# Two visits to half-size TensorE tiles per group of four batches become one

## The chip, the cores and the metric

The kernel runs on one core of a Trainium2 chip. A time is the device time of one launch in microseconds (us), the median of several runs; less is better. A core has five engines that work side by side, each through its own queue of instructions in the order of the program: TensorE (PE; its weight loads are listed as PEld), VectorE (DVE), ScalarE (ACT), GpSimd (POOL) and SyncE (SP), which here issues every DMA. Engines wait for each other with semaphores. TensorE writes into PSUM, which has eight banks; VectorE and ScalarE empty them.

## The reference

`x` is 128 batches of 128 nodes with 512 features, `adj` a 128 x 128 weighted adjacency matrix. Two layers follow each other, each with a residual. All is fp32.

```python
# layer 0
h = relu(layernorm(x))
x = x + (adj @ h) @ L0_weight + L0_bias
# layer 1: attention of 8 heads of 64, masked where adj == 0
h = relu(layernorm(x))
q, k, v = split(h @ w_qkv)
attn = softmax(where(adj == 0, -inf, q @ k.T * 64 ** -0.5))
o = (attn @ v) @ w_proj + b_proj
x = x + o + layernorm(o) * gamma + beta
```

## The kernel before

**Two phases.** Phase 1 (`phase1`, L479) does layer 0 for all batches and puts x1 and x1 + beta into DRAM. Phase 2 (`phase2_group`, L569) does layer 1 in 32 groups of four batches, each group two pairs. Weight products are made of three fp32r matmuls (high part, low part, correction) for precision: `times_weights` (L449) has 12 matmuls of 128x512 for one batch, and writes two PSUM banks, a and b.

**A group of phase 2** has on TensorE:
- qk (L594): eight blocks of 12 matmuls over all four batches; ScalarE (L601) and VectorE (L602) bring banks a and b together into `qk` tiles;
- v: 12 matmuls for each batch (L455 with `wv`), emptied at L629 and L630;
- scores (L651): 8 fp32 matmuls for each batch with a contraction of 64, so two row halves of the array work side by side. They fill two banks for each batch. VectorE adds the mask (L660) and takes maxima (L665), ScalarE the exponentials (L672), VectorE the reciprocals (L677), GpSimd divides (L678);
- the probabilities go to DRAM and back with rows exchanged (`exchange`, L521), and VectorE transposes blocks (L703);
- attend (L721): 8 fp32 matmuls for each batch with 64 output rows, two column halves of the array; one bank for each batch;
- `split_left` (L441) cuts an attend bank into three parts (ScalarE L443, VectorE L444 and L445), and proj multiplies them: 12 matmuls for each batch (L455 with `wA`); then bias, layernorm and residual, and a store.

The attends of a group take place in the next group. Scores and attends both use the array in halves. Before, each group goes to half-size tiles twice: attends of the older group's first pair with scores of this group's first pair, then, later in the group, the same for the second pairs. `rests` holds what is left to do for each pair: `rest_of` gives the read-back, transposes, attend, proj and the tail of the layer.

**The next group's hidden states** are fetched meanwhile (`fetch`, L537): read x1, statistics, relu (L553), to DRAM and back, transposes (L557), then the three parts on ScalarE (L560, L563) and GpSimd (L561, L564). There are six places for batches in `hp`.

**What sets the order.** Every operation goes into a planner (`Plan`, L57) with its engine, an assumed duration, the buffers it reads and writes, and a wanted time: `at` for TensorE, `due` for the others. The planner runs a list schedule: an engine that is free takes the available operation with the earliest wanted time for which a buffer slot is free, and instructions are emitted in that order. Operations with `tiled=True` are those in half-size tiles: the planner favours staying in the present mode (`stay`) and adds `turn` at a change. Slots are places in SBUF (`t`, `f`) or PSUM banks (`b0` to `b7`, taken by anything named `ps`). `s` (scores) and `pT` (transposed probabilities) share four places f0 to f3. `T4` is the period of a group assumed for the wanted times; `t0` is the start of one. `rank` counts pairs from the end: ranks 1 and 0 are the last group's, rank 0 transposes its probabilities on TensorE (L709) rather than through DRAM, and both use a plain fp32 proj (L740).

Of the kernel before, what the change touches and what calls it, by code (L numbers as in the profile page):

```python
# [52 lines left out]
class Op:  # L53
    __slots__ = ("eng", "us", "fn", "at", "due", "prio", "bufs", "preds", "succ", "n", "ready", "start", "end", "id", "lands", "what", "tiled", "early")


class Plan:  # L57
# [10 lines left out]
    def op(self, eng, us, fn, r=(), w=(), at=None, due=None, lands=None, what="", after=(), tiled=False, early=0.0):  # L68
        o = Op()
        o.eng, o.us, o.fn, o.at, o.due, o.lands, o.what, o.tiled = eng, us, fn, at, due, lands, what, tiled  # L70
        o.early = early
# [30 lines left out]
    def schedule(self):  # L102
# [22 lines left out]
        while len(order) < len(self.ops):  # L125
# [6 lines left out]
            for e in self.ENGINES:  # L132
# [7 lines left out]
                for item in sorted(avail[e], key=lambda i: (i[0] - (stay if self.ops[i[1]].tiled == tiled else 0.0), i[1])):  # L140
                    o, taken = self.ops[item[1]], []
                    if held and any(b.slots in held for b in o.bufs if b.slots and not b.name):
                        continue
# [68 lines left out]
def kernel(  # L212
# [36 lines left out]
    def named(prefix, *numbers):  # L249
# [8 lines left out]
        "qk": group(named("t", 0, 8)), "v": group(named("t", 8, 14)), "op": group(named("t", 14, 18)),  # L258
# [182 lines left out]
    def split_left(p, name):  # L441
        h, l, s = (buf(name, [P, C, P], HALF) for _ in range(3))
        op("ACT", 0.53, lambda: nc.scalar.activation(h.ap, p.ap, AF.Copy, scale=CUT), r=[p], w=[h], what=name + "h")  # L443
        op("DVE", 0.63, lambda: nc.vector.tensor_tensor(l.ap, p.ap, h.ap.bitcast(F32), op=ALU.subtract), r=[p, h], w=[l], what=name + "l")  # L444
        op("DVE", 0.63, lambda: nc.vector.scalar_tensor_tensor(s.ap, h.ap.bitcast(F32), UP, p.ap, op0=ALU.mult, op1=ALU.subtract),  # L445
           r=[p, h], w=[s], what=name + "s")
        return h, l, s

    def times_weights(parts, w, at, what):  # L449
# [7 lines left out]
        for m, (p, start, stop) in enumerate(((a, True, False), (a, False, True), (b, True, True))):  # L457
            op("PE", 0.91, lambda p=p, m=m, start=start, stop=stop: run(p, m, start, stop), r=[parts[m][:2], w], w=[p], at=at + 0.91 * m, what=what)
# [62 lines left out]
    def exchange(src, w, kb, what):  # L521
        d = in_dram([P, Q, w], f"d{w}")
        dma(lambda: d.ap, lambda: src(), kb, r=[src.b], w=[d], what=what + " out")

        def land(dst, after=()):
            for q in range(Q):
                dma(lambda q=q: dst()[q * R:(q + 1) * R, :, :], lambda q=q: d.ap[:, q, :].rearrange("(n r) w -> r n w", n=Q),
                    kb / 4, r=[d], w=[(dst.b, q)], what=what + " in", after=after)
# [40 lines left out]
    def phase2_group(j):  # L569
# [3 lines left out]
        at_qk = (0.0, 2.8, 8.4, 11.2, 16.8, 19.6, 22.4, 25.2)  # L573
        at_v = (31.7, 34.5, 42.9, 45.7)
        at_t = (28.0, 48.5)
        at_p = (37.3, 40.1, 52.3 + 5.6, 52.3 + 14.0)
        if not left:
            at_v, at_t = (31.7, 34.5, 46.6, 49.4), (28.0, 37.3)
        for p in range(2):
            fetch(group[2 * p:2 * p + 2], t0 - (37, 8)[p])  # L580
# [6 lines left out]
        for g in range(8):  # L587
# [15 lines left out]
            if g == 4:  # L603
                gate = [b.writers[-1][1]]
        V = {}

        def scores(p):
            pair = group[2 * p:2 * p + 2]
            at_scores = t0 + at_t[p] + 1.8
# [3 lines left out]
            if rank < 4:  # L613
                last = START2 + T4 * (B // 4 - 1)
                at_attend = [last + d for d in ((66.9, 67.9), (57.8, 57.8), (37.3, 37.3), (28.0, 28.0))[rank]]
                at_proj = [last + d for d in ((69.0, 72.5), (60.0, 63.6), (52.2, 55.0), (41.0, 43.8))[rank]]
            S, last = scores_of(pair, place, QK, rank, at_scores)
            rests.append(lambda gate: rest_of(pair, V, rank, S, at_attend, at_proj, gate))
            final[:] = [last]
            return [last]  # L620

        if rests:
            rests.pop(0)(gate)
        scores(0)
        for n, i in enumerate(group):
            v = V[i] = buf("v", [P, D])
            tv = t0 + at_v[n]
            a, b = times_weights([(HP[i, m], None, part(i, m)) for m in range(3)], wv, tv, "v")
            op("ACT", 0.53, lambda v=v, a=a: nc.scalar.activation(v.ap, a.ap, AF.Copy, scale=UP), r=[a], w=[v], due=tv + 1, what="vA")  # L629
            op("DVE", 0.63, lambda v=v, b=b: nc.vector.tensor_tensor(v.ap, b.ap, v.ap, op=ALU.add), r=[b], w=[v], due=tv + 2, what="vB")  # L630
        if len(rests) > 1:
            rests.pop(0)(gate)
        scores(1)
# [6 lines left out]
    def scores_of(pair, place, QK, rank, at_scores):  # L640

        S = []
        for n, i in enumerate(pair):
            ts = at_scores + 1.0 * n
            ps = [buf("ps", [P, C, P]) for _ in range(2)]
# [13 lines left out]
            for e in range(2):  # L659
# [3 lines left out]
                   r=[ps[e], maskb], w=[(s, e)], due=ts + 1 + n, what="mask")  # L663
            mx = buf("mx", [P, 2 * H])
            op("DVE", 1.15, lambda heads=heads, mx=mx: nc.vector.tensor_reduce(mx.ap[:, :H], heads(), AX.XY, ALU.max),  # L665
               r=[s], w=[mx], due=ts + 4 + 4 * n, what="max")
            op("ACT", 0.2, lambda mx=mx: nc.scalar.mul(mx.ap[:, :H], mx.ap[:, :H], -scale), w=[mx], due=ts + 5 + 5 * n, what="mx")  # L667
# [5 lines left out]
            for g in range(4):  # L673
                op("ACT", 0.79, lambda g=g, exps=exps: exps((2 * g, 2 * g + 1)), r=[(mx, "m")], w=[(s, ("e", g)), (mx, g)],
                   due=ts + 6 + 2.3 * g + 9.2 * n if rank > 1 else ts + 4 + 1.2 * g + 4 * n, what="exp")
            if rank:
                op("DVE", 0.18, lambda mx=mx: nc.vector.reciprocal(mx.ap[:, H:], mx.ap[:, H:]), w=[mx], what="rec", due=ts + (15 + 9.2 * n if rank > 1 else 9 + 4 * n))  # L677
# [3 lines left out]
                   r=[mx], w=[s], what="div", due=ts + (16 + 9.2 * n if rank > 1 else 10 + 4 * n))  # L681
# [9 lines left out]
            land = exchange(View(s, lambda ap: ap), H * R, 512, "e") if rank else None  # L691
# [3 lines left out]
    def rest_of(pair, V, rank, S, at_attend, at_proj, gate):  # L695

        PT = []
        for n, (s, heads, land) in enumerate(S):
            pT = buf("pT", [P, Q, 2 * C, R])
            PT.append(pT)  # L700
            if rank:
                land(View(pT, lambda ap: ap.rearrange("p q h r -> p q (h r)")), gate)
# [13 lines left out]
        def attend(some):  # L716
            for n in some:
# [100 lines left out]
```

## Time and profile before

| | |
|---|---|
| median of 3 runs | 2150.61 us (2149.41 to 2150.62) |
| profiled execution | 2148.78 us, span of its instructions 2147.0 us |
| TensorE busy | 2135.3 us, granted clock 0.999 |
| VectorE, ScalarE, GpSimd busy | 1723.9, 1484.8, 1529.3 us |
| first qk of phase 2 | 475.9 us after the start of the span |
| one group in the steady part | 51.74 us |

Busy time is the union of an engine's instructions. The page also follows the chain of work that ended last, back from the last instruction, and gives its shares by engine and line. A timeline row has start in us from the start of the span, length in us, engine, line, operation, output<-inputs by the program's names, shape and count; instructions of one kind that follow each other are one row. In brackets stands the engine's idle time before it and what ended it. A row of busy times by stretch has, for each engine, the time in which it worked in this stretch and the number of its instructions. An fp32 matmul leaves two records, an fp32r matmul one. Ends of matmuls are modelled; starts of weight loads show the pace better.

### The profile page before, as it was taken

The page shows a single profiled execution, that of the slowest core. Times are in us where ns is not written, and L with a number is a line of the kernel's source. Part 1 is how long each engine was busy: PE and PEld are TensorE (multiplying, and loading weights), DVE is VectorE, ACT ScalarE, POOL GpSimd, SP SyncE. Part 2 cuts the span into 40 slices and gives each one's busy share as a digit, 9 for nine tenths or more (in the row PEclk, how much of TensorE's full clock was granted, in tenths as well). Part 3 has the DMA queues.
Part 4 walks back from the last instruction along what each step waited for, and adds up shares of the span by engine and source line. Part 5 has one row for each costly group of instructions (what it writes and reads, how often), then busy time and mean ns, then how long its engine had stood idle before and what let it go on. Part 6 is the DMA issues. An engine that isn't in the chain of part 4 may idle for free.

```text
span 2147.0 us, 40973 instructions
## 1 busy us (share of the span) xinstructions
PE 2135.3 (99%) x12819; PEld 1781.8 (83%) x12819; DVE 1723.9 (80%) x3279; ACT 1484.8 (69%) x4238; POOL 1529.3 (71%) x1278
## 2 busy tenths in 40 slices
PE   9999999999999999999999999999999999999998
PEld 7888888888888888888888888888888888888885
DVE  7889888886787887787777787777777777777778
ACT  7778778767766666676666666666666666666654
POOL 7888878784666666677777777777777777777655
PEclk9999999999999999999999999999999999999999
DMA  7676666665666666566666666666666666666653
GB/s 241 220 243 227 229 220 226 224 237 163 190 191 185 188 182 179 177 177 177 177 177 177 187 177 179 186 186 195 186 195 185 185 187 185 185 185 184 186 166 108
DMA packets 297865, 410.71 MB, mean 191 GB/s; under 512 B 33072, under 2 KB 163248, under 8 KB 297648
## 3 DMA queue, kind: packets, MB, share of 16 engines
q1 hardware_dynamic: 297648, 408.09, 62.6%
q8 instruction: 102, 1.67, 0.3%
q14 instruction: 115, 0.94, 0.2%
HBM read 207.68 MB, written 200.28 MB: 190 GB/s over the span
## 4 chain that ended last, share of the span: by engine, by line
PE 96%; DVE 1%; DMA 1%; SPq 1%; issue 0%; POOL 0%; ACT 0%; POOLq 0%; DVEq 0%; ACTq 0%
PE b L455 47%; PE b L594 32%; PE b L651 6%; PE b L721 5%; PE b L497 5%; PE b L506 1%; SPq L280 1%; DMA f<-d 0%; DMA f<-in_x_dram 0%; DVE t L756 0%; DMA out_dram<-t 0%; DMA t<-in_x_dram 0%; DVE n L665 0%; DVE t L466 0%; POOL m L397 0%
## 5 line engine op out<-in xcount | busy, mean ns | idle before, releaser
L455 PE MATMUL b<-wA,t 128*128 128x512 f32 x2976 | 732.6, 393 | 1.2 <-DVE t L444 0.8
L594 PE MATMUL b<-hp,wqk 128*128 128x512 f32 x3072 | 715.4, 390 | 0.0
L594 PEld LDWEIGHTS b<-hp,wqk 128*128 128x128 f32 x3072 | 574.3, 188 | 122.1
L455 PEld LDWEIGHTS b<-wA,t 128*128 128x128 f32 x2976 | 549.6, 188 | 110.2 <-DVE t L444 1.0
L561 POOL TENSOR_TENSOR hp<-t,hp 128x512 fp32r<-128x512 f32 x128 | 165.6, 1305 | 400.1 <-ACT hp L560 370.7
L672 ACT ACTIVATE f<-f,n 128x128 f32<-128x128 f32 x1024 | 397.7, 391 | 3.1
L455 PE MATMUL b<-wv,hp 128*128 128x512 f32 x1536 | 378.1, 392 | 0.0
L455 PEld LDWEIGHTS b<-wv,hp 128*128 128x128 f32 x1536 | 285.8, 188 | 62.3
L602 DVE TENSOR_TENSOR t<-b,t 128x512 f32<-128x512 f32 x256 | 175.2, 685 | 137.7 <-PE b L594 74.2
L678 POOL TENSOR_TENSOR f<-f,n 128x1024 f32<-128x1024 f32 x126 | 241.7, 1922 | 57.3 <-DVE n L677 52.2
L601 ACT ACTIVATE t<-b 128x512 f32<-128x512 f32 x256 | 151.4, 592 | 163.4 <-PE b L594 162.9
L444 DVE TENSOR_TENSOR t<-b,t 128x512 fp32r<-128x512 f32 x248 | 168.3, 679 | 64.1 <-ACT t L443 62.8
L672 ACT ACTIVATION_READ_ACCUMULATOR f<-f,n 128x1 f32 x1024 | 194.6, 190 | 0.0
L667 ACT ACTIVATE n<-n 128x8 f32<-128x8 f32 x128 | 26.0, 203 | 241.7 <-DVE n L665 241.7
L703 DVE STREAM_TRANSPOSE f<-f 128x1024 f32<-128x1024 f32 x126 | 156.2, 1239 | 41.0 <-DMA f<-d 37.5
L748 POOL TENSOR_TENSOR t<-t,t 128x512 f32<-128x512 f32 x126 | 164.3, 1304 | 28.7 <-DVE t L466 26.3
L660 DVE TENSOR_TENSOR f<-b,maskb 128x512 f32<-128x512 f32 x256 | 163.7, 680 | 21.7 <-PE b L651 21.7
L443 ACT ACTIVATE t<-b 128x512 fp32r<-128x512 f32 x248 | 144.8, 584 | 47.6 <-PE b L497 42.1
L564 POOL TENSOR_TENSOR hp<-hp 128x512 fp32r<-128x512 f32 x128 | 166.3, 1300 | 5.0
L445 DVE SCALAR_TENSOR_TENSOR t<-t,b 128x512 fp32r<-128x512 f32 x248 | 167.4, 675 | 0.0
L751 POOL TENSOR_TENSOR t<-t,gamma_b 128x512 f32<-128x512 f32 x122 | 158.6, 1300 | 6.0 <-ACT t L750 2.8
L752 POOL TENSOR_TENSOR t<-t,t 128x512 f32<-128x512 f32 x122 | 158.4, 1299 | 5.0
(123 smaller groups left out, 3259.1 us busy)
## 6 DMA issues: line engine op xcount, KB each, us to landing
d<-f SPq DMA_DIRECT2D x126, 512.0 KB, 3.5
f<-d SPq DMA_DIRECT2D x504, 128.0 KB, 4.1
t<-x1d SPq DMA_DIRECT2D x128, 256.0 KB, 3.9
d<-t SPq DMA_DIRECT2D x128, 256.0 KB, 3.7
t<-d SPq DMA_DIRECT2D x512, 64.0 KB, 3.5
t<-x1b SPq DMA_DIRECT2D x128, 256.0 KB, 4.2
out_dram<-t SPq DMA_DIRECT2D x128, 256.0 KB, 3.1
t<-in_x_dram SPq DMA_DIRECT2D x91, 256.0 KB, 3.0
```

The source lines that it names most:

```text
L444: op("DVE", 0.63, lambda: nc.vector.tensor_tensor(l.ap, p.ap, h.ap.bitcast(F32), op=ALU.subtract), r=[p, h], w=[l], what=name + "l")
L445: op("DVE", 0.63, lambda: nc.vector.scalar_tensor_tensor(s.ap, h.ap.bitcast(F32), UP, p.ap, op0=ALU.mult, op1=ALU.subtract), r=[p, h], w=[ ...
L455: nc.tensor.matmul(p.ap, lhsT=parts[m][2]()[:, c], rhs=w.ap[:, m, c, :], start=start and c == 0, stop=stop and c == C - 1)
L561: op("POOL", 1.35, lambda ht=ht, h=h, l=l: nc.gpsimd.tensor_tensor(l(), ht(), h().bitcast(F32), op=ALU.subtract), r=[h1, HP[i, 0]], w=[HP[ ...
L564: op("POOL", 1.38, lambda l=l, s=s: nc.gpsimd.tensor_tensor(s(), s().bitcast(F32), l().bitcast(F32), op=ALU.subtract), r=[HP[i, 1]], w=[HP ...
L594: nc.tensor.matmul(p.ap, lhsT=wqk.ap[:, which, c, col:col + P], rhs=hp[:, pick, :, which, c, :], start=start and c == 0, stop=stop and c = ...
L602: op("DVE", 0.63, lambda r=r, b=b: nc.vector.tensor_tensor(r.ap, b.ap, r.ap, op=ALU.add), r=[b], w=[r], due=tg + (4 if g < 7 else 2), what ...
L660: op("DVE", 0.62, lambda e=e, heads=heads, ps=ps: nc.vector.tensor_tensor(heads()[:, e * C:(e + 1) * C], ps[e].ap.rearrange("p c (q r) -> ...
L672: nc.scalar.activation(v[:, h], v[:, h], AF.Exp, bias=mx.ap[:, h:h + 1], scale=scale, accum_out=mx.ap[:, H + h:H + h + 1])
L678: op("POOL", 1.93, lambda heads=heads, mx=mx: nc.gpsimd.tensor_tensor(heads().rearrange("p h q r -> p q h r"), heads().rearrange("p h q r ...
L748: op(eng, us, lambda x1=x1, o=o, unit=unit: unit.tensor_tensor(x1.ap, x1.ap, o.ap, op=ALU.add), r=[o], w=[x1], due=tl + (3 if rank > 1 els ...
L751: op("POOL", 1.32, lambda o=o: nc.gpsimd.tensor_tensor(o.ap, o.ap, gamma_b.ap, op=ALU.mult), r=[gamma_b], w=[o], due=tl + 7, what="gamma")
```

## The change

- **One visit for each group.** In `phase2_group` all attends of the older group (four batches) are put ahead of all scores of this one (four batches). `rest_of` now returns its transposed tiles and a function `finish`; every attend in the plan names all four tiles (`also`).
- The planner takes attends batch by batch, ((0,), (1,)), instead of pair by pair.
- **Wanted times.** qk at an even 2.74 us, then the visit, then v and proj alternating by batch. Due times of masks, maxima, exponentials, divisions, DRAM exchange and splits are set anew; the group j == 1 fetches its second pair with a due time 4 us earlier.
- **Urgent.** Masks (except of the last three pairs) and the splits of the first pair's attends are `urgent`: no other operation starts on their engine if it would still run when they become ready.
- **Slots.** `v` has four places instead of six; the three parts of `op` have two places each instead of four together; v takes its place before its matmuls.
- The reads from DRAM (`land`) lose the gate that held them behind the fifth qk block, and get a due time.

```diff
@@ class Plan, schedule
                     if held and any(b.slots in held for b in o.bufs if b.slots and not b.name):
                         continue
+                    if not o.urgent and any(r < t + o.us and self.ops[i].urgent for r, i in pending[e]):
+                        continue
@@ slots
-        "qk": group(named("t", 0, 8)), "v": group(named("t", 8, 14)), "op": group(named("t", 14, 18)),
+        "qk": group(named("t", 0, 8)), "v": group(named("t", 8, 12)), "oph": group(named("t", 12, 14)), "opl": group(named("t", 14, 16)), "ops": group(named("t", 16, 18)),
@@ def times_weights
-            op("PE", 0.91, ..., r=[parts[m][:2], w], w=[p], at=at + 0.91 * m, what=what)
+            op("PE", 0.91, ..., r=[parts[m][:2], w, *into], w=[p], at=at + 0.91 * m, what=what)
@@ def exchange
-                    kb / 4, r=[d], w=[(dst.b, q)], what=what + " in", after=after)
+                    kb / 4, r=[d], w=[(dst.b, q)], what=what + " in", after=after, due=due and due + 3)
@@ def phase2_group
-        at_qk = (0.0, 2.8, 8.4, 11.2, 16.8, 19.6, 22.4, 25.2)
-        at_v = (31.7, 34.5, 42.9, 45.7)
-        at_t = (28.0, 48.5)
-        at_p = (37.3, 40.1, 52.3 + 5.6, 52.3 + 14.0)
+        at_qk = [2.74 * g for g in range(8)]
+        at_v = (29.2, 34.7, 40.2, 45.7)
+        at_t = (22.0, 23.8)
+        at_p = (31.9, 37.4, 42.9, 48.4)
...
-            fetch(group[2 * p:2 * p + 2], t0 - (37, 8)[p])
+            fetch(group[2 * p:2 * p + 2], t0 - (37, 8 if j != 1 else 12)[p])
...
-        if rests:
-            rests.pop(0)(gate)
+        late = [rest() for rest in rests]
+        rests.clear()
+        for _, finish in late:
+            finish([pT for PT, _ in late for pT in PT])
         scores(0)
+        scores(1)
         for n, i in enumerate(group):
...
-            a, b = times_weights([(HP[i, m], None, part(i, m)) for m in range(3)], wv, tv, "v")
+            a, b = times_weights([(HP[i, m], None, part(i, m)) for m in range(3)], wv, tv, "v", [v])
...
-        if len(rests) > 1:
-            rests.pop(0)(gate)
-        scores(1)
@@ def scores_of
-                   r=[ps[e], maskb], w=[(s, e)], due=ts + 1 + n, what="mask")
+                   r=[ps[e], maskb], w=[(s, e)], due=ts + (1 + n if rank < 3 else -26), what="mask", urgent=rank > 2)
@@ def rest_of
-        for some in ((0, 1),) if rank else ((0,), (1,)):
-            att = op("PE", 0.83 * len(some), ..., r=[V[pair[n]] for n in some] + [PT[n] for n in some],
+            for some in ((0,), (1,)):
+                att = op("PE", 0.83 * len(some), ..., r=[V[pair[n]] for n in some] + [PT[n] for n in some] + list(also),
...
-                parts = split_left(PO[n], "op")
+                    parts = split_left(PO[n], "op", at_attend[n] - 24 if p == 0 else at_attend[n] + 6, p == 0)
```

## The prediction

> **What bounds the kernel now.** I read the busy shares and the chain of waits on the page first, to see which engine sets the end.
>
> ```profile
> PE 2135.3 (99%) x12819; PEld 1781.8 (83%) x12819; DVE 1723.9 (80%) x3279; ACT 1484.8 (69%) x4238; POOL 1529.3 (71%) x1278
> ...
> PE 96%; DVE 1%; DMA 1%; SPq 1%; issue 0%; POOL 0%; ACT 0%; POOLq 0%; DVEq 0%; ACTq 0%
> ```
>
> TensorE is busy 99% of the span, and 96% of the chain runs on it. A busy TensorE isn't one at its peak, so next came the busy time by stretch for one steady group (first attend to first attend), and the weight loads around one visit, whose starts show the pace that the matmul ends, being modelled, do not.
>
> ```profile
> core 0: us, PE busy (x) PEld busy (x) DVE busy (x) ACT busy (x) POOL busy (x), PEclk, DMA share, GB/s
> 1002.85:1054.59 51.74, 51.74 (x321) 43.06 (x320) 40.84 (x75) 35.33 (x109) 36.45 (x30) 1.00 0.62 182
> ```
>
> ```profile
> 1002.08 0.41 PEld L455 LDWEIGHTS b<-wv,hp 128*128 128x128 f32 x2
> 1002.85 1.73 PEld L721 LDWEIGHTS b<-f,t 128*64 128x64 f32 x32 [0.35 <-DVE m L433]
> 1004.74 1.86 PEld L651 LDWEIGHTS b<-t,t 64*128 64x128 f32 x32 [0.17 <-issue]
> 1006.73 0.99 PEld L455 LDWEIGHTS b<-wv,hp 128*128 128x128 f32 x5
> ```
>
> A group takes 51.74 us, at full clock, while VectorE works 40.8, ScalarE 35.3 and GpSimd 36.5. The visit is the two middle rows: 32 loads for the attends of two batches, 32 for the scores of two (each fp32 matmul leaves two records). The pace of full-array matmuls comes from the longest pieces of the chain:
>
> ```profile
> 476.07 21.76 PE b L594 x96
> ```
>
> 21.76/96 = 0.2267 us each. The 192 full matmuls of a group (96 qk, 48 v, 48 proj) make 43.52 us, so two visits cost 51.74 - 43.52 = 8.22, or 4.11 each.
>
> **What one visit less is worth.** Within a visit, attends step at 0.109 us a pair of loads, scores at 0.112 (from the starts of single loads). Eight pairs are a batch: 0.874 for an attend, 0.894 for a score. Four of such are 3.54 us a visit; the rest of 4.11, 0.57, is switching. The same from the starts: last full load to first attend 0.540 where 0.227 is the pace, attend to score 0.308 for 0.109, score to full 0.309 for 0.112. That is 0.71 too late, less 0.12 because the second full load comes 0.11 after the first, less 0.05 for a short first step: **0.54**. Between 0.54 and 0.58 I take 0.56 us. All matmuls stay; in the built order of the changed kernel each steady group reads 96 qk, 32 attends, 32 scores, then four times 12 v and 12 proj. Groups 1 to 30 each lose one visit: 30 x 0.56 = **16.8 us gained**, if nothing new waits.
>
> **Does the double visit fit into eight PSUM banks?** It writes 4 attend and 8 score banks. I walk its clock from the first attend load (0): last loads of attends 0 and 1 at 0.72 and 1.59; scores begin at 3.64, 4.54, 5.43, 6.32; first v load at 7.42. A consumer that waits starts 0.41 to 0.43 after the last load (read at the first mask and first split of visits). The changed order of VectorE is: split of attend 0 (two operations), of attend 1 (two), then all eight masks. The step is half of a pair of masks:
>
> ```profile
> 1006.11 1.27 DVE L660 TENSOR_TENSOR f<-b,maskb 128x512 f32<-128x512 f32 x2
> 1007.42 1.22 DVE L665 TENSOR_REDUCE n<-f 128x8 f32<-128x1024 f32 x1
> ```
>
> about 0.60 us, starts overlapping. ScalarE's first halves end at 1.72 and 2.59; the splits run 1.75 to 4.23, so attend banks 0 and 1 are free at 3.03 and 4.23, ahead of score 2 at 5.43. Masks start at 4.84, end at 5.52, 6.12, 6.72, 7.32 and so on to 9.72. Score 3 (6.32) takes the two of score 0 (6.12 plus the semaphore: spare about 0.1), v (7.42) the next. No stall.
>
> Here a rule speaks against the change. The Trainium skill, TensorEngine Tiling, section PSUM Bottleneck, warns that packing small matmuls speeds up TensorE but not the emptying of PSUM, so the copies may become the limit. If all masks had to end before v, TensorE would wait 9.72 - 7.42 = 2.3 us in each visit: +69 us over 30 groups, a kernel slower by some 50. The rows say that only splits 0 and 1 and four masks must be done by then; I take nothing. The cover is thin: with it gone, each late microsecond beyond the spare costs 30 us.
>
> **The other edits in the steady group.** Splits of attends 2 and 3 wait for proj 0 and 1 to free their operand slots (two of each kind now); ScalarE stands at that wait from about 11.2 to 11.5, exponentials, relus and hidden-state copies queued behind. Added waits make `v` take its slot before its matmuls (four slots, not six), behind attends that are done by then: nothing. Counts of DMAs and of work on VectorE, ScalarE and GpSimd are unchanged; SP's landing reads lose the gate on a qk matmul and take due times. The longest chain is the next hidden states. Their relus end at 15.8 and 16.6 (after the first batch's eight exponentials, 3.09 us as in the tail), and then come store, read-back and transpose:
>
> ```profile
> 518.21 1.51 ACT L553 ACTIVATE t<-t,m 128x512 f32<-128x512 f32 x2
> ...
> 528.36 0.70 DVE L557 STREAM_TRANSPOSE t<-t 128x512 f32<-128x512 f32 x1
> 530.02 0.71 DVE L557 STREAM_TRANSPOSE t<-t 128x512 f32<-128x512 f32 x1 [0.96 <-DMA t<-d]
> ```
>
> The second relu ends at 519.7, its transpose starts 10.3 us later, waiting for the read-back itself. So it starts at 26.9, the second copy ends on ScalarE at 28.3, and the next qk wants it at 29.2: spare 0.9. GpSimd's low halves end at 29.7, wanted at 31.0. The fourth softmax ends near 30.6, its division at 34.2, its read-back is issued at 38 and lands at 43.6, transposed by 46.2, wanted at about 53.8. Nothing is late; cost 0, bound +1 us a group if that copy slips by 2.
>
> **Start.** Group 0 now sends four batches of scores at once.
>
> ```profile
> 499.57 2.06 PE L651 MATMUL b<-t,t 64*128 64x128 f32 x32
> 501.56 9.37 PE L455 MATMUL b<-wv,hp 128*128 128x512 f32 x40
> ...
> 536.64 1.97 PE L721 MATMUL b<-f,t 128*64 128x128 f32 x32
> ```
>
> Scores end at 503.3, 40 v matmuls at 512.4. Eight masks from 500.77 push the first maximum to 505.7, exponentials to 507.1; two batches (6.3), a v copy and two hidden-state copies stand ahead in ScalarE's queue until 515.4. The first qk matmul of group 1 needs the last of these: 3.1 us idle. qk ends at 537.2, attends start at 537.8. Before it was 536.64 with four v matmuls (0.91) already done, 535.73 like for like: **2.1 us lost**, between 0 (if copies come first) and 4.
>
> **Tail.** Counted from the first attend load of the last group (like for like 2087.73), the old end is 59.3 us later. The new order: visit to 7.42, the last v/proj 0.65 late since each maximum stands between the masks (VectorE's order differs here), 96 full matmuls to 29.8, two attends to 32.0, flips, plain proj to 39.5, flips to 40.9, an attend to 41.8. The last attend needs a flip copied by VectorE behind 17 operations of the former two batches. The same operations took 10 us in the old tail, from the first to the end of the last of these rows:
>
> ```profile
> 2121.28 0.69 DVE L463 SCALAR_TENSOR_TENSOR t<-b,bp_b 128x512 f32<-128x512 f32 x1 [2.66 <-POOL t L752]
> ...
> 2130.44 0.95 DVE L756 SCALAR_TENSOR_TENSOR t<-t,l,t 128x512 f32<-128x512 f32 x1
> ```
>
> Starting at 33.6, they let the copy end at 44.1. TensorE waits 2.4, ends at 52.2, and 8.45 us of last stage (2138.55 to 2147.0 before) make 60.7: **1.4 us lost**, between -1 and +4.
>
> **Sum.** 2147.0 - 16.8 + 2.1 + 1.4 = 2133.7 as span. The profiled execution took 2148.78, 1.8 around its span; the median shown is 2150.61. Taken off that: 2150.6 - 13.3 = **2137.3 us**, 0.6% faster.
>
> **Rivals.**
> (a) As summed: 2134 to 2141. Chance 0.55.
> (b) The edges cost nothing: ScalarE and VectorE keep up at start and end, so 31 visits go, 2150.6 - 17.4 = 2133. For it: before, TensorE hardly idles in either. Against: queues are in order and the orders name the blockers. 0.15.
> (c) Small new waits of 0.1 to 0.4 us a group, most likely at score 3 (spare 0.1) or at the next qk (0.9): 30 x 0.25 = 7.5 given back, 2145. 0.19.
> (d) The waits eat the gain within 0.2% (0.3 to 0.6 us a group), 2149. 0.04.
> (e) Slower: the hidden-state copy is late at qk. Store and read-back must land within 10 us of relu; each group pays lateness minus 0.9. Break-even is 13.3/30 + 0.9 = 1.35 us late; at 2.5 late, +48: 2185. For it: before, some relu-to-transpose times are 12 to 13 us (there the transposes stood in queue, data landed). Against: DMA is 62% busy. 0.07.
> That another engine bounds (the change then does nothing) I rule out: VectorE's 40.8 of 51.2 leaves 10 us.
>
> **How the numbers follow.** (a) is likeliest: 2137.3. Its own range 2134 to 2141; reaching 2131 takes in (b), 2145 half of (c): about 0.8. A measurement of this kernel can tell 0.2%, 4.3 us, from no change. Faster by more: (a), (b) and nearly all of (c), 0.88; same: (d) and a rest of (c), 0.05; slower 0.07.
>
> **What would show it.** Right: 32 visits instead of 64, each with 64 attend loads then 64 score loads, the switch gaps still 0.54, 0.31, 0.31; group period 51.2; TensorE idle near 512 to 515 and once in the last 20 us. Wrong: a period of 51.5 or more, with waits of score loads on masks (c), or of qk on the hidden-state copy or GpSimd's halves (e); no idle stretch at 512 (b); switches that cost more where four attends follow each other.

## The result, and the profile after

| | before | after |
|---|---|---|
| median of all executions beside each other, us | 2150.32 (4; 2149.41 to 2150.62) | 2136.95 (4; 2133.6 to 2137.72) |
| ratio, with 95% interval | | 0.9936 (0.9918 to 0.9953) |
| profiled execution: time, us | 2148.78 | 2133.6 |
| profiled execution: span, us | 2147.0 | 2131.6 |
| one steady group, us | 51.74 | 51.17 |
| visits to half-size tiles | 64 | 32 |

The change makes the kernel 0.64% faster: 13.4 us by the medians, 15.2 by the two profiled executions. (Lines after L440 carry other numbers in the changed kernel: the masks are L657, attends L719, scores L648, qk L594, v and proj L457, hidden-state copies L562.) The busy times and the chain on the page of the changed kernel:

```profile
PE 2117.0 (99%) x12819; PEld 1782.8 (84%) x12819; DVE 1731.4 (81%) x3279; ACT 1476.8 (69%) x4238; POOL 1523.5 (71%) x1278
...
PE 98%; DVE 1%; issue 0%; ACT 0%; SPq 0%; DMA 0%; POOL 0%; POOLq 0%; ACTq 0%; DVEq 0%
```

The same 12819 matmul records, in 18.3 us less of TensorE time; TensorE still sets the end. The stretch from one first attend to the next (columns: stretch and length, then busy time and instructions of each engine, granted clock, DMA), and the weight loads around its visit:

```profile
997.62:1048.79 51.17, 51.17 (x321) 43.09 (x320) 41.25 (x74) 34.90 (x109) 36.21 (x31) 1.00 0.61 186
```

```profile
996.86 0.41 PEld L594 LDWEIGHTS b<-hp,wqk 128*128 128x128 f32 x2
997.62 3.47 PEld L719 LDWEIGHTS b<-f,t 128*64 128x64 f32 x64 [0.35 <-ACT t L601]
1001.27 3.65 PEld L648 LDWEIGHTS b<-t,t 64*128 64x128 f32 x64 [0.17 <-issue]
1005.04 0.99 PEld L457 LDWEIGHTS b<-wv,hp 128*128 128x128 f32 x5
```

One visit with 64 attend records and 64 score records stands where two of 32 and 32 stood. The gaps between the starts of the loads are what they were, 0.540 into the attends, 0.308 from attends to scores, 0.309 out. The list of all waits of TensorE (total, number, longest, in us) has none between the first attends of groups 1 and 31; it is, in full:

```profile
PE b L594 <- ACT hp L562: 2.5, 1, 2.5
PE b L719 <- DVE f L710: 1.6, 1, 1.6
PE b L323 <- POOL t masks.py:199: 1.4, 1, 1.4
PE b L499 <- ACT t L491: 0.5, 1, 0.5
PE b L457 <- DVE f L657: 0.5, 1, 0.5
```

The first is the start of the second phase (qk of group 1 waits for the hidden-state copy), the second the last attend (it waits for the flip copied by VectorE), the last the v matmul of the last group. The third and the fourth belong to the first phase. In the timeline of TensorE:

```profile
514.99 6.20 PE L594 MATMUL b<-hp,wqk 128*128 128x512 f32 x26 [2.51 <-ACT hp L562]
...
2112.81 1.09 PE L719 MATMUL b<-f,t 128*64 128x128 f32 x16
2115.48 1.09 PE L719 MATMUL b<-f,t 128*64 128x128 f32 x16 [1.58 <-DVE f L710]
```

One thing does not fit. The other executions of the same kernel took 2136.7 to 2137.7, with spans of 2134.8 to 2135.7: 3 to 4 us more than the profiled one, while before, nine executions beside the first experiments lay within 2148.5 and 2150.8 and the profiled one 1.5 below the median. So the experiments ask two things: whether the steady gain is what the prediction says it is, and what happens at the ends, in the executions that the first profile does not show.

### The profile page after: what moved, and what is told of

Same layout as the page of the kernel before. It is cut to its first block, busy times and chain, and to the rows that moved or that the text cites. A ratio compares the mean times of both kernels' runs of the same rounds, so it can differ in the third digit from the quotient of the medians.

```text
span 2131.6 us, 40786 instructions
## 1 busy us (share of the span) xinstructions
PE 2117.0 (99%) x12819; PEld 1782.8 (84%) x12819; DVE 1731.4 (81%) x3279; ACT 1476.8 (69%) x4238; POOL 1523.5 (71%) x1278
## 4 chain that ended last, share of the span: by engine, by line
PE 98%; DVE 1%; issue 0%; ACT 0%; SPq 0%; DMA 0%; POOL 0%; POOLq 0%; ACTq 0%; DVEq 0%
PE b L457 48%; PE b L594 33%; PE b L719 5%; PE b L648 5%; PE b L499 5%; PE b L508 1%; PE b L738 0%; ACT f L669 0%; DVE f L657 0%; SPq L282 0%; DMA t<-in_x_dram 0%; DVE n L662 0%; DVE t L754 0%; DVE t L740 0%; DVE m L393 0%
## 5 line engine op out<-in xcount | busy, mean ns | idle before, releaser
L457 PE MATMUL b<-wA,t 128*128 128x512 f32 x2976 | 727.1, 393 | 0.1
L594 PE MATMUL b<-hp,wqk 128*128 128x512 f32 x3072 | 701.6, 389 | 2.5 <-ACT hp L562 2.5
L594 PEld LDWEIGHTS b<-hp,wqk 128*128 128x128 f32 x3072 | 576.6, 188 | 122.5 <-ACT hp L562 2.9
L457 PEld LDWEIGHTS b<-wA,t 128*128 128x128 f32 x2976 | 549.9, 188 | 108.5 <-DVE t L447 0.6
L457 PE MATMUL b<-wv,hp 128*128 128x512 f32 x1536 | 373.1, 392 | 0.5 <-DVE f L657 0.5
L457 PEld LDWEIGHTS b<-wv,hp 128*128 128x128 f32 x1536 | 285.9, 188 | 62.9 <-DVE f L657 0.7
L563 POOL TENSOR_TENSOR hp<-t,hp 128x512 fp32r<-128x512 f32 x128 | 164.6, 1293 | 25.3 <-DMA t<-x1b 13.4
L657 DVE TENSOR_TENSOR f<-b,maskb 128x512 f32<-128x512 f32 x256 | 156.4, 680 | 19.3 <-PE b L648 19.3
L555 ACT ACTIVATE t<-t,m 128x512 f32<-128x512 f32 x128 | 97.1, 807 | 91.4 <-DVE m L435 91.4
```

Of the source, the lines that this page charges most:

```text
L457: nc.tensor.matmul(p.ap, lhsT=parts[m][2]()[:, c], rhs=w.ap[:, m, c, :], start=start and c == 0, stop=stop and c == C - 1)
L563: op("POOL", 1.35, lambda ht=ht, h=h, l=l: nc.gpsimd.tensor_tensor(l(), ht(), h().bitcast(F32), op=ALU.subtract), r=[h1, HP[i, 0]], w=[HP[ ...
L594: nc.tensor.matmul(p.ap, lhsT=wqk.ap[:, which, c, col:col + P], rhs=hp[:, pick, :, which, c, :], start=start and c == 0, stop=stop and c = ...
```

## The experiments

Times are compared with the changed kernel (2136.9) and with the kernel before, which ran beside each. In e5 to e8 two lines are added, so the later ones stand two further down (masks L659, divisions L677, attends L721).

### e1 and e9: the changed kernel again

No edit. Expected of e1:

> The changed kernel itself, not altered, for its interval and for why its executions lay between 2133.6 and 2137.7 us while the profiled one had a span of 2131.6. Theory A (the 2.5 us for which TensorE has nothing to do at 512.5 to 515.0 us let the granted clock fall for a while behind it in most executions): a median of 2136 to 2138, and an execution whose profile shows 0.5 in the clock row near 515 to 520 where its time is over 2136. Theory B (the spread comes from the transfers of the first phase, or from anything not at that place): the same median, but a profile of 2136 or more shows full clock there and its extra time before 500 us.

Measured: 2136.91 (2133.62 to 2137.86), before 2149.89; ratio 0.9938 (0.9925 to 0.9952). This time the profiled execution is one of the longer ones, with a span of 2135.0. TensorE at the start, and two stretches there, the wait and what follows it:

```profile
517.01 23.63 PE L594 MATMUL b<-hp,wqk 128*128 128x512 f32 x96 [2.51 <-ACT hp L562]
540.57 3.71 PE L719 MATMUL b<-f,t 128*64 128x128 f32 x64
```

```profile
513.57:516.98 3.41, 0.93 (x5) 0.43 (x3) 1.14 (x3) 3.41 (x15) 2.98 (x2) 1.00 0.27 109
516.98:520.39 3.41, 3.38 (x8) 2.70 (x9) 0.20 (x1) 3.41 (x17) 3.10 (x4) 0.50 0.69 238
```

The column before the DMA share is the granted clock: 0.50 for 3.41 us, beginning where qk begins after its wait, and full again behind it. Only 8 matmuls fit into it; in the first profile of the changed kernel such a stretch, behind the same wait of 2.51 us, has the full clock and 15:

```profile
515.00:518.40 3.40, 3.40 (x15) 2.82 (x16) 0.20 (x1) 3.40 (x17) 3.11 (x4) 1.00 0.66 233
```

From the first qk load to the first attend load it is 23.56 us in e1 and 21.99 in the first profile: the stretch at half clock costs 1.57. The spans differ by 3.45. The rest comes earlier: qk starts at 517.01 instead of 514.99, because the first phase ended 2.02 later; 0.14 is won back in the first period (51.17 for 51.31). So both theories hold in part.

The same kernel ran once more, beside e8 on one chip:

> The changed kernel once more, not altered, beside e8 on one chip: a median of 2136 to 2138.5. From what the first repeat showed (qk of group 1 started 2.0 us later than in the first profile, and took 1.57 us more in a stretch of 3.41 us at half clock): an execution with a mean clock of 0.998 is 1.5 to 2 us longer than one of 0.999 with the same first phase, and the rest of the spread, about 2 us, is the first phase's.

Measured: 2136.84 (2136.21 to 2138.15); the profiled execution has a span of 2135.0 again, with half clock from 516.9 to 520.3, and 23.46 us from the first qk load (517.10) to the attends (540.56). So two of three profiles of the changed kernel have this stretch. The mean clock, rounded to three digits, doesn't sort all executions (one of 0.999 took 2137.68), so how often it comes beyond those three is open; what decides it within them stands in the last section. The profile of the kernel before has full clock from 4.7 us to the tail.

### e3: one part of the change undone

The change gave the second pair of group 1 a fetch of its own, 12 us ahead; here it is 8, as in all groups.

```diff
-            fetch(group[2 * p:2 * p + 2], t0 - (37, 8 if j != 1 else 12)[p])
+            fetch(group[2 * p:2 * p + 2], t0 - (37, 8)[p])
```

> One part of the change undone: the second pair of group 1 is fetched 8 us ahead of the group, as in all others, instead of 12. The copies come in ScalarE's queue after the exponentials of batch 2 and one more v copy, so qk of group 1 starts about 518.8 instead of 515.0: 6.4 us idle instead of 2.5. Theory B: 3.8 us longer than the changed kernel, 2137.5 profiled and 2140.5 to 2141 as the median. Theory A: the clock row shows 0.5 after 518 in the profile, and the kernel is 5 to 7 us longer than the changed one's best time, 2139 to 2141, in every execution, so that they lie close together.

Measured: 2140.64 (2139.44 to 2141.85), 3.7 us above the changed kernel. The wait of qk is 6.21 us, predicted 6.4:

```profile
520.03 24.18 PE L594 MATMUL b<-hp,wqk 128*128 128x512 f32 x96 [6.21 <-ACT hp L562]
```

```profile
517.80:524.60 6.80, 4.57 (x11) 3.60 (x12) 2.34 (x4) 6.80 (x28) 5.83 (x5) 0.50 0.94 277
```

Two stretches of 3.41 us at half clock, part of them in the wait itself; from qk to attends 24.11 us. All five executions have a mean clock of 0.998 or 0.997. The clock row is that of theory A. The median fits both (theory A's 5 to 7 above the changed kernel's best time is 7.0 here, theory B said 2140.5 to 2141), and the narrow spread of theory A did not come, so only the clock row decides. Against e1, which had a drop too, the span is 3.6 longer: 3.70 for the longer wait and 0.55 from qk to attends, less 0.68 for an earlier first phase. So the edit that the change made for group 1 is worth 3.7 us.

### e2: the copies earlier

```diff
-            fetch(group[2 * p:2 * p + 2], t0 - (37, 8 if j != 1 else 12)[p])
+            fetch(group[2 * p:2 * p + 2], t0 - (37, 8 if j != 1 else 22)[p])
```

> The due time of the second pair's fetch in group 1 goes from 12 to 22 us ahead of the group, so that ScalarE makes both hidden-state copies after two heads of batch 1 (about 511 to 512.7 us) instead of after batch 1 and the v copy (513.7 to 514.9). Everything agrees that qk of group 1 then starts near 512.7 instead of 515.0, with about 0.25 us idle instead of 2.5; of these 2.3 us up to 0.5 can be lost again at the fourth attend, whose transposed softmax lands at 537.9 now: span 2129.3 to 2129.8, where the profiled one of the changed kernel was 2131.6. Theory A (idle time pulls the clock down in most executions): the executions also come together, median 2131 to 2132.5, 4 to 6 us under the changed kernel's. Theory B (spread from elsewhere): the median is only 1.8 to 2.3 us lower, about 2134.5 to 2135, and the executions lie as far apart as before.

Measured: 2137.37 (2136.48 to 2137.72), the same as the changed kernel (2136.91); neither theory's time. The idle at the head of qk did go, but:

```profile
513.84 9.45 PE L594 MATMUL b<-hp,wqk 128*128 128x512 f32 x40 [0.29 <-ACT hp L562]
524.91 13.07 PE L594 MATMUL b<-hp,wqk 128*128 128x512 f32 x56 [1.61 <-ACT t L628]
541.99 1.09 PE L719 MATMUL b<-f,t 128*64 128x128 f32 x16 [1.25 <-DMA t<-d]
```

In the middle of qk TensorE waits 1.61 us for a v copy (L628): the copies of v stand behind the exponentials on ScalarE, and they free PSUM banks that qk needs. Then the fourth attend waits 1.25 us for the last softmax, which its transpose gets too late, and the first group's period is 54.43 instead of 51.31. The copies were put ahead of other work on ScalarE, which in this trace works without a pause from 507.6 to 530.3, so the wait moved. The clock does what the first theory says: no listed wait is longer than 1.7 (2.24 from load to load), the profile shows full clock from 6.5 us to the tail, and all five executions lie within 1.3 us at 0.999.

### e4: the visit split between attends and scores

```diff
-        at_v = (29.2, 34.7, 40.2, 45.7)
+        at_v = (25.6, 34.7, 40.2, 45.7)
...
-            at_scores = t0 + 25.6 + 1.8 * p
+            at_scores = t0 + 29.0 + 1.8 * p
```

> The merged visit is taken apart along the other line: in each group four attends, then the twelve matmuls of the first v, then the four scores; all else as in the changed kernel. If each switch has its own price, as the gaps in the trace say (full to attend 0.540 for a pace of 0.227, attend to score 0.308 for 0.109, score or attend to full 0.309 for 0.112 less 0.12 from the next step), a group gains an attend-to-full switch (0.08) and a full-to-score switch (0.31) and loses an attend-to-score switch (0.20): 0.19 us for each of some 31 groups, 5.9 us longer than the changed kernel. If what counts is a visit as a whole (0.56 us each, whatever is in it): 0.56 x 31 = 17 us longer, back at the time before the change. If the switches are covered and the gain came from waits: no difference.

Measured: 2169.12 (2167.32 to 2169.8), ratio to before 1.009 (1.0076 to 1.0103): 32 us longer than the changed kernel, more than any of the three theories. The loads of one group:

```profile
958.38 3.47 PEld L719 LDWEIGHTS b<-f,t 128*64 128x64 f32 x64 [0.35 <-ACT t L601]
962.03 2.59 PEld L457 LDWEIGHTS b<-wv,hp 128*128 128x128 f32 x12 [0.17 <-issue]
964.97 2.98 PEld L648 LDWEIGHTS b<-t,t 64*128 64x128 f32 x50 [0.35 <-issue]
968.10 0.96 PEld L648 LDWEIGHTS b<-t,t 64*128 64x128 f32 x14 [0.16 <-DVE f L657]
...
988.13 3.59 PEld L594 LDWEIGHTS b<-hp,wqk 128*128 128x128 f32 x16
992.19 0.77 PEld L594 LDWEIGHTS b<-hp,wqk 128*128 128x128 f32 x4 [0.47 <-ACT t L628]
```

The gaps are the known ones: 0.308 from attends to v, 0.540 from v to scores, 0.309 out. So the switches have about the price they were given: by all starts 0.23 a group more, 0.19 expected, 7.0 us between the first attends of groups 1 and 31. What the expectation missed is the banks. The v that now comes first holds two of the eight when the scores begin, so the last score waits for a mask (a step of 0.35 where 0.112 is the pace), and at the other end qk waits for a bank that ScalarE's v copy frees (a step of 0.64 for 0.227 in 28 groups). The scores take 13.3 us longer in all, 7.1 of them at this step, and qk loses 12.4. With the switches that makes 32.7, which is all that is lost in these 30 groups. Why the scores lose the other 6.2, in two single steps of 0.11 us in each group, is open. So the experiment confirms the price of a switch, and shows that what stands next to the visit cost over three times as much here.

### e5: the maxima between the masks

In groups 1 to 30 VectorE takes each batch's maximum right behind its two masks. The planner's cost of that maximum is set low so that TensorE's order stays.

```diff
+            apart = 2 < rank < 62
+            turn = at_scores - 1.8 * p - 26 + 3 * (2 * p + n)
...
-                   r=[ps[e], maskb], w=[(s, e)], due=ts + (1 + n if rank < 3 else -26), what="mask", urgent=rank > 2)
+                   r=[ps[e], maskb], w=[(s, e)], due=turn if apart else ts + (1 + n if rank < 3 else -26), what="mask", urgent=rank > 2)
...
-            op("DVE", 1.15, lambda heads=heads, mx=mx: nc.vector.tensor_reduce(mx.ap[:, :H], heads(), AX.XY, ALU.max),
-                r=[s], w=[mx], due=ts + 4 + 4 * n if rank < 2 else tb + 1, what="max")
+            op("DVE", 0.05 if apart else 1.15, lambda heads=heads, mx=mx: nc.vector.tensor_reduce(mx.ap[:, :H], heads(), AX.XY, ALU.max),
+                r=[s], w=[mx], due=turn + 1.4 if apart else ts + 4 + 4 * n if rank < 2 else tb + 1, what="max", urgent=apart)
```

> In the steady groups 1 to 30 VectorE takes the maximum of a batch right behind its two masks (mask, mask, max, four times), instead of all eight masks first; TensorE's order and everything else stay. This tests whether the eight PSUM banks suffice only because of VectorE's order. If they do: the last group of the changed kernel already has this order and its v waits 0.55 us for a mask there; so a period of 51.7 to 51.8 instead of 51.17, v waiting on a mask in each of 30 groups, 16 to 20 us longer than the changed kernel, 2153 to 2157, slower than before the change. If the banks have slack (the rival: VectorE's order does not matter): within 2 us of the changed kernel, 2135 to 2139.

Measured: 2205.67 (2204.39 to 2209.39), ratio to before 1.0254 (1.0239 to 1.027): 69 us longer than the changed kernel. The waits of TensorE:

```profile
PE b L594 <- ACT hp L562: 37.7, 30, 2.8
PE b L457 <- DVE f L659: 17.2, 31, 0.7
```

The second line is what was asked: v waits for a mask in each group, by the gaps of the loads 0.62 us in the median of 30 groups, 18.8 us in all, as expected. So the banks suffice only because the masks come first.

The first line was not expected. With the planner's other choices (it now thinks VectorE has more time) the hidden-state copy comes late at the next qk, by 1.54 us in the median, 46.3 us in all by the gaps. In the changed kernel this copy ends 1.02 us before qk's first load (median of 29 groups), in e5 0.05 before it: the spare is gone. That part is not the price of the maxima alone, since the plan moved with them; how much is which was not separated.

18.8, 46.3, 4.1 within qk, where four stretches at half clock lie, and 1.8 elsewhere make the 71.0 by which the two profiles differ between the first attends of groups 1 and 31. Of two waits, the one before qk at 785.2 has a drop (its second row is the stretch behind it), the longer one before qk at 1053.0 (here cut in two) has none:

```profile
782.24:785.65 3.41, 1.61 (x8) 1.03 (x7) 2.38 (x5) 2.70 (x5) 2.57 (x2) 1.00 0.80 240
785.65:789.07 3.42, 3.42 (x10) 2.65 (x9) 1.46 (x3) 2.42 (x6) 3.42 (x4) 0.50 0.97 323
1048.48:1051.89 3.41, 2.35 (x11) 1.62 (x9) 1.11 (x3) 1.75 (x3) 3.19 (x4) 1.00 0.61 168
1051.89:1055.31 3.42, 2.31 (x10) 1.91 (x11) 2.22 (x4) 2.96 (x6) 3.17 (x3) 1.00 0.97 348
```

This kernel is a test bench for the clock: of its 31 waits of TensorE before a qk, the seven with 2.40 us or more from load to load have four drops behind them, the 24 shorter ones none. Length alone does not sort the seven (2.41 has a drop, 2.78 and 3.13 have none); the last section says what does.

### e6 and e7: the first group's maxima early, and the tail's flip copy

If the start is bound by ScalarE's chain, it should begin sooner. In group 0 alone (the lines of e5 with another `apart`, the cost of the maximum as it was) the order mask, mask, max lets the first exponentials start 3.5 us earlier; the fetch is put 20 us ahead.

```diff
+            apart = rank >= 62
...
-            fetch(group[2 * p:2 * p + 2], t0 - (37, 8 if j != 1 else 12)[p])
+            fetch(group[2 * p:2 * p + 2], t0 - (37, 8 if j != 1 else 20)[p])
```

> The same order, mask, mask, max, in group 0 alone, where the softmax of four batches keeps ScalarE busy, and the second pair of group 1 fetched 20 us ahead of the group. The first exponentials then start at 503.1 instead of 506.6, both hidden-state copies come behind the second batch's exponentials and are done at 512.1, before TensorE ends the v matmuls at 512.5; the last batch's exponentials end at about 520.4 instead of 522.9. If the start is bound by the beginning of ScalarE's chain: no idle TensorE at 512.5, qk of group 1 at 512.5 instead of 515.0, attends near 534.4 without a wait, full clock in every execution, so a span near 2129.5 and a median of 2131 to 2132.5, 4.5 to 6 us below the changed kernel. Rival (as when the copies alone were moved: each wait taken away comes back as another): a wait of 1 to 2.5 us on a v copy or on the last transposed softmax takes its place, 2134 to 2136.

Measured: 2138.65 (2136.28 to 2140.08), beside before at 2150.82; ratio 0.994 (0.9927 to 0.9952), no gain over the changed kernel (0.9938 in e1). The rival's wait came, on the last transposed softmax; the median is still longer than the rival's 2134 to 2136, and two of the five executions have a mean clock of 0.998, which the profile, at full clock, does not explain. TensorE goes from v into qk without a listed wait, and then:

```profile
540.07 1.09 PE L721 MATMUL b<-f,t 128*64 128x128 f32 x16 [1.88 <-DMA t<-d]
...
544.91 0.38 PE L648 MATMUL b<-t,t 64*128 64x128 f32 x2 [0.74 <-DVE t L447]
```

The fourth attend waits for the last softmax, the scores behind it for banks that the late splits free: the first period is 55.52 instead of 51.31. GpSimd tells why. Its queue had one division (L677), four subtractions for the hidden states, then the other three divisions in a row, so that three exchanges of 512 KB went out together:

```profile
512.52 1.92 POOL L677 TENSOR_TENSOR f<-f,n 128x1024 f32<-128x1024 f32 x1 [13.78 <-DVE n L676]
514.40 2.54 POOL L563 TENSOR_TENSOR hp<-t,hp 128x512 fp32r<-128x512 f32 x2
516.90 2.54 POOL L566 TENSOR_TENSOR hp<-hp 128x512 fp32r<-128x512 f32 x2
519.40 5.67 POOL L677 TENSOR_TENSOR f<-f,n 128x1024 f32<-128x1024 f32 x3
```

In e7 the same start is joined with one edit in the tail, on VectorE's copy of the last batch's flip:

```diff
-... r=[flips[0]], w=[(pT, 0)], what="pT")
+... r=[flips[0]], w=[(pT, 0)], what="pT", due=at_attend[0] - 20, urgent=True)
```

> The edit of the first group as in e6, and at the other end VectorE's copy of the last batch's flipped softmax is due early and marked urgent, so that it goes ahead of three to four normalisation steps of other batches (2.3 us). TensorE's order stays. If the last attend waits only for that copy (1.58 us): it starts with no wait or up to 0.3, and from the first attend load of the last group to the end 58.0 to 58.3 instead of 59.5, so 1.2 to 1.6 us below e6. If the end hangs on VectorE's own work, which is only re-ordered: 59.5 as now, the same time as e6.

Measured: 2138.6 (2135.26 to 2140.36), the time of e6. In its trace the last attend waits no more:

```profile
2117.46 1.97 PE L721 MATMUL b<-f,t 128*64 128x128 f32 x32
```

and the end comes 58.44 us after the last group's first attend load, instead of 59.45 in e6: 1.0 us, of 1.2 to 1.6 expected. So the edit works, but is worth less than the wait it takes away, and less than the executions differ.

### e8: GpSimd's divisions in time

The edits of e7, and the first two divisions and all reciprocals of group 0 go ahead:

```diff
-                ... what="rec", due=tb + 7 if rank > 1 else ts + 9 + 4 * n)
+                ... what="rec", due=turn + 3 if rank > 62 else tb + 7 if rank > 1 else ts + 9 + 4 * n, urgent=apart)
...
-                    r=[mx], w=[s], what="div", due=tb + 8 if rank > 1 else ts + 10 + 4 * n)
+                    r=[mx], w=[s], what="div", due=turn + 3 if rank > 62 else tb + 8 if rank > 1 else ts + 10 + 4 * n)
```

> The edits of e7, and in addition GpSimd divides the first two batches of group 0 as soon as their exponentials are there, ahead of the hidden-state subtractions. In e6 and e7 GpSimd made one division at 512.5, then four subtractions, and the other three divisions in a row from 519.4 to 525.1; the three exchanges then left SP's queue within 4 us, the last softmax landed at 538.8, and the fourth attend waited 1.9 us for it. If that order is what moved the wait: divisions near 508, 510, 517.6 and 520.7, the last exchange leaves at 522.6 instead of 525.1, the fourth attend (537.5) does not wait; qk of group 1 starts near 512.9 with about 0.4 us idle, attends near 534.8, period to the next group 51.2 to 51.4 instead of 55.7; the end as in e7 (58.4 after the last group's attends); full clock; span 2128 to 2129.5, median 2130.5 to 2132.5, 4.5 to 6.5 us below the changed kernel. Rival: the landings are late because the transfers compete, whatever the order: 1 to 2 us of wait at the fourth attend again, a median of 2134 to 2137.

Measured: 2133.65 (2131.28 to 2134.26), ratio to before 0.9919 (0.9906 to 0.9933). The changed kernel on the same chip (e9) took 2136.84; its fastest execution, 2136.21, is above e8's slowest. So e8 is the best of all kernels here, 3.2 us below the changed one. The profiled execution had a late first phase (first score load at 502.49; 499.34 in the first profile of the changed kernel), so its times are read from there. Its median is 1.2 us above the expected 2130.5 to 2132.5; less that late start of 3.15, the profiled span of 2131.7 lies within the expected 2128 to 2129.5. TensorE and GpSimd at the start:

```profile
516.08 22.07 PE L594 MATMUL b<-hp,wqk 128*128 128x512 f32 x96 [0.45 <-ACT hp L562]
538.08 3.71 PE L721 MATMUL b<-f,t 128*64 128x128 f32 x64
```

```profile
511.32 1.92 POOL L677 TENSOR_TENSOR f<-f,n 128x1024 f32<-128x1024 f32 x1 [10.18 <-DVE n L676]
513.83 1.92 POOL L677 TENSOR_TENSOR f<-f,n 128x1024 f32<-128x1024 f32 x1 [0.59 <-DVE n L676]
515.71 2.54 POOL L563 TENSOR_TENSOR hp<-t,hp 128x512 fp32r<-128x512 f32 x2
518.22 2.54 POOL L566 TENSOR_TENSOR hp<-hp 128x512 fp32r<-128x512 f32 x2
520.72 1.91 POOL L677 TENSOR_TENSOR f<-f,n 128x1024 f32<-128x1024 f32 x1
523.51 1.92 POOL L677 TENSOR_TENSOR f<-f,n 128x1024 f32<-128x1024 f32 x1 [0.88 <-DVE n L676]
```

Less 3.15, the divisions stand at 508.2, 510.7, 517.6 and 520.4, as expected; the attends start without a wait, the first period is 51.28, the end 58.42 after the last group's attends. From the first score load to the end it is 1629.2 us, against 1632.2 in the first profile of the changed kernel and 1633.6 in that of e9: 2.05 at the start, 1.0 in the tail, and the stretch at half clock that e9 has and e8 hasn't. All five executions have 0.999.

## Why the prediction was right, and where

It said 2137.3 and 0.6% faster; 2136.95 and 0.64% came. The mechanism is right: one visit less in each group, no new wait between them, and idle time at the two places that were named. That the total is so close is partly luck, since several terms are off and cancel.

- **What one visit less is worth: right.** 0.56 us taken, 0.58 measured (the groups' medians are 51.747 and 51.167), 17.4 us in 30 groups instead of 16.8. Like for like the 30 groups gain 17.8, because one of the kernel before had a wait that is gone (its period is 52.24) and the first one after is 0.14 longer. The gaps and the paces within the pieces did not change, so nothing else gained in these groups; e4 shows nearly the same prices where a visit is split.
- **Eight banks suffice by VectorE's order: right.** No load waits in groups 1 to 30. Masks start 4.84 us after the first attend load (1002.46 less 997.62), the walked 4.84. "The cover is thin" was right too: with the maxima in between, v waits 0.62 us a visit in e5; with a v ahead, the scores lose 0.44 and qk 0.41 a group in e4. If v had needed all masks to end first, each visit would have cost 2.3; no trace here shows such a wait.
- **The next hidden states with 0.9 us to spare: right.** 1.02 measured in the median, 0.25 in the tightest group. What the slower rival (e) would cost is shown by e5: the copy comes about 2.5 us later for TensorE, 1.54 beyond the spare, and costs 46.3 us of its 71; (e) had put 48 on a copy 2.5 late. The cause of the lateness there is the plan.
- **Start: mechanism right, two sizes off, one part missing.** The place and the waiter are the named ones; the idle time is 2.51 us, not 3.1, and attends start at 536.98, not 537.8. The like-for-like of 535.73 is a slip: by 536.64 the kernel before had done eight v matmuls more than the changed one, not four. Between its first scores and the attends stand 40 and two times 4, where the changed kernel has 40; the weight loads of the kernel before show the two:

```profile
512.84 0.76 PEld L455 LDWEIGHTS b<-wv,hp 128*128 128x128 f32 x4
535.42 0.87 PEld L455 LDWEIGHTS b<-wv,hp 128*128 128x128 f32 x4
```

  So like for like it is 536.64 - 1.81 = 534.83, and 2.15 us are lost. That 2.1 had been said is luck: 0.8 too much in the start of the attends, 0.9 too little in the count. What the prediction left out is the clock: in two of three profiles this wait is followed by 3.41 us at half clock, 1.57 us more.
- **Tail: mechanism right, size off.** v waits 0.55 (0.65 predicted). The last attend waits 1.58, not 2.4, and the end stands at 59.4, not 60.7, so under 0.2 is lost, not 1.4. Two terms were mis-sized: the flip copy ends 43.3 after the first attend load, not 44.1 (the operations in front of it took less), and the last stage after TensorE's end takes 7.9, not 8.45.
- **Sum and median.** By the profile the terms are 2147.0 - 17.8 + 2.15 + 0.2 = 2131.6, as measured, 2.1 below the predicted span; 1.0 of that is the steady part and 1.2 the tail. The median lay 1.8 above the profiled execution before, and the prediction kept that; after, it lies 3.35 above, because the first profile shows an execution without the drop of the clock and with an early first phase. 2.1 too much and 1.5 too little nearly cancel. Rival (b), "the edges cost nothing" (2133), is nearest to the profiled execution alone, but not for its reason: the idle stretch at 512 is there.

## What to carry to other kernels

Take the price of a switch between tile sizes from the starts of weight loads, and then ask which PSUM bank each load of the merged visit needs and what VectorE does just before: here the same masks and maxima in another order cost 18.8 us, more than the merged visits save. An idle gap that an edit opens on TensorE may cost more than its length, and one execution may not show it: look at the clock in a second profile, and at how the gap lies on the clock's windows (below). A wait at the start of a pipeline goes only when the whole chain behind it is moved (e8); moving one operation in a full queue moves the wait (e2, e6).

## What the runs showed that was not expected

- **The clock falls after short waits, if enough of a wait lies in one window.** In each of the eleven profiles the clock changes only at whole multiples of 3.413 us after its first rise: in e1 after 150, 151 and 623 of them, in e5 at nine such places. The rows of e1 and e5 above are windows of this grid; these two are the first profile's around the same wait:

```profile
510.15:513.57 3.42, 2.33 (x11) 1.59 (x9) 1.84 (x4) 3.42 (x17) 1.92 (x1) 1.00 0.00 0
513.57:516.98 3.41, 1.99 (x9) 1.65 (x10) 0.69 (x1) 3.41 (x15) 3.35 (x3) 1.00 0.56 225
```

  Here the grid cuts the wait of 2.51 us into 1.09 and 1.42 us of idle time, and the clock stays full. In e1 2.48 of it lie in one window, in e9 2.30, and the next window runs at half clock. Over all eleven profiles, every window with 2.1 us or more of idle TensorE is followed by one at half clock, and at full clock none with 1.66 or less is. Between 1.80 and 1.91 it goes either way (three falls in e5; none in three other windows, two of them in a tail), and the ends of matmuls, from which idle time is read, are modelled. In e3 and e4 the fall lasts two windows; in e4 the first of them had only 0.63 us of idle time, and why the clock stayed down there is open. So the same wait costs 1.57 us more or not, by where the grid lies, and the grid lies differently from execution to execution. An estimate from these numbers: a wait of 2.5 us at a random place puts 1.8 us or more into one window in about two of three cases. The Trainium skill, TensorE: Matmul & The Clock Gate, section What's actually happening, has a window of 3413 ns that runs freely, and a fall to half clock after at least one idle window. The grid agrees with the window and with its running freely. But no window needed to be idle throughout: 1.80 to 2.48 us were enough, so here the measurement decides.
- **The first phase differs by up to 3 us between executions.** The first qk load of the second phase came between 475.2 and 478.6 us in eleven profiles of nine kernels whose first phase is the same work, and between 475.2 and 477.5 in e1 to e4, which ran on one chip. Why is not shown. Differences of this size in one profile say nothing about a change in the second phase; counting from the first score load leaves them out.
